# A two-layer graph kernel on one core: X W's table in partition order, fewer early rows of A, and other cuts of two strip loads

## The chip, the cores and the metric

The kernel runs on one core of a Trainium2 chip. The metric is the time of one execution on the device in microseconds (us); the median of several runs is taken. A profiled execution gives the trace that the tables and rows below come from.

The engines have short names in all views: PE is TensorE (matmuls), DVE is VectorE, ACT is ScalarE, POOL is GpSimd and SP is SyncE. Loads and stores are issued by an engine's queue (POOLq, SPq, ACTq) and carried out by 16 DMA engines.

## The reference

There are N = 2708 nodes with D = 128 features, and A is the 0/1 adjacency matrix. Layer 0 adds a diffusion and an attention over cosine similarities, and layer 1 is a graph attention in which the softmax-like weights are normalised by a product with A:

```python
# layer 0
deg = clip(A.sum(1), 1);  dis = deg ** -0.5
diffusion = (dis[:, None] * A * dis[None, :]) @ x - x
attn = softmax(beta * cos(x, x) * A, axis=1)
x = layernorm(x + diffusion + sigmoid(alpha) * (attn @ x - x))
# layer 1
XW = X @ W
s_col, s_row = XW @ a[0, :128], XW @ a[0, 128:]
den = exp(leaky_relu(s_row[:, None] + s_col[None, :], 0.01))
num = A @ den
att = where(num != 0, den / num, 0)
H = A @ (att @ XW)
out = layernorm(X + layer1)      # layer1 = H
```

Everything is float32. The kernel gets x, A (`adj`) and A transposed (`adj_t`), with rows padded with zeros to 2816.

## The kernel before, in words

The nodes are cut into `NB` = 22 blocks of 128 rows, and the columns of A into `NS` = 6 strips of `SW` = 512, of which the last, strip 5, is 148 wide. The work goes through five stages in the trace's time: the attention of layer 0 (0 to 217 us), the diffusion (217 to 306), scores and tables (306 to 362), the main loop (362 to 575), and H with the output (575 to 681).

**The diffusion.** The loop runs over the strips in the order 0, 5, 1, 2, 3, and strip 4 follows behind it. `diffuse` multiplies one strip by x, block by block. Strips 1 to 4 (`RAISED`) are multiplied by two rounded parts of x (`x_hi`, `x_lo`), strips 0 and 5 by `x_sb`, the tile that holds x. Behind each strip come the layernorm, two scores (`sb_ps`), and small work on DVE that tallies them. A strip is loaded by `load_strip` in two DMAs of 11 blocks each, strips 1 to 4 on POOL's queue and strips 0 and 5 on SP's. There are three rooms: `strip_a` holds strips 0, 2 and 4 in turn, `strip_b` strips 1 and 3, and `strip_c` strip 5. So strip s + 2 is loaded once `diffuse(s)` has ended.

**The sums over rows of A.** Separately, `tot` collects sums over the rows of A with weights that come from the scores. The first three strips' columns (`KEPT`) are no longer at hand when the weights are known, so those columns are loaded again, 768 KB for each block of rows; this is `first_strips`, with 12 matmuls for each block. The other columns are read from the strips that remain (`kept_strips`). `fill` with a pattern of "e" (first) and "k" (kept) places such blocks of work by hand between other work on PE. The tiles for "e" rotate through five rooms: the room of x (`x_sb`), and those of the four halves of `x_hi` and `x_lo`. Three early blocks have a pool of their own, `early_nat`, and are summed behind the strips 1, 2 and 3; a fourth, in `x_sb`, follows behind strip 3.

**The order of the instructions.** Up to the end of the diffusion, a scheduler at build time orders the instructions of each engine. From `strict.append("end of the diffusion")` on, PE, DVE, ACT and POOL keep the written order (`pinned`).

**The tables.** `project` makes X W, and `store_xw` writes it to a scratch table in device memory (`xw_d`, one row of 128 numbers for each node) in two DMAs on ACT's queue. The nodes are sorted into up to `NG` = 24 groups of `G` = 126. One-hot products (`onp`, `k_ons`, `j_ons`, `tab_ps`) turn the order into lists of row numbers: `k_no` for the rows of A and `j_no` for the rows of X W. A list's values are sums in which an absent entry is 0, so each number carries an offset (`from_n`) that `rows_of_table` takes off again. `gather(g)` then loads the rows of A of group g by an indirect DMA on POOL's queue, into a ring of four rooms of which the first is `x_sb` again, and `gather_xw(g)` loads the rows of X W.

**The main loop** runs over the groups: a product (`num`), a logarithm, a division, a power, and a product that collects `m_acc`. Then H = A·M is made in rounded parts. A slower path for other data (`general`) is in the program and is not executed.

Of the kernel before, what the change touches and what calls it, by code (L numbers as in the profile page):

```python
# [9 lines left out]
F32 = mybir.dt.float32  # L10
# [4 lines left out]
ALU = mybir.AluOpType  # L15
# [3 lines left out]
P = 128  # L19
N = 2708  # L20
D = 128
NB = (N + P - 1) // P
NP = NB * P
LAST = N - (NB - 1) * P
SW = 512
# [7 lines left out]
NG = 24  # L33
# [4 lines left out]
LAG = 2  # L38
TAIL = (NS - 1) * SW
PARTS = ((0, 1024), (1024, 2048), (TAIL, N), (2048, TAIL))  # L40
EARLY_ROWS = 3
RAISED = (1, 2, 3, 4)
KEPT = 3
LIMIT = 16.0
# [5 lines left out]
def grouped(  # L50
# [14 lines left out]
    nc = tc.nc  # L65

    def pool(name, bufs=1, space=None, side="left", stack=ctx):
        kw = {"space": space} if space else {}
        return stack.enter_context(
            tc.tile_pool(name=name, bufs=bufs, side=side, reuse_waits="tile", **kw)  # L70
        )
# [4 lines left out]
    def width(s):  # L76
        return min(SW, N - s * SW)

    def blocks(s):
        return min(SW // P, NB - s * (SW // P))  # L80
# [35 lines left out]
    def counted(name, pattern, base, step, size):  # L116
        t = const.tile([P, size], F32, name=name)
        nc.gpsimd.iota(
            t, pattern, base=base, channel_multiplier=step,
            allow_small_or_imprecise_dtypes=True,  # L120
        )
        return t
# [12 lines left out]
    nc.gpsimd.memset(going[:, :, 0], 0.0)  # L135
    pad = const.tile([P, NB], F32, name="pad")
    from_n = const.tile([P, NB], F32, name="from_n")
    after_node = const.tile([P, 2], F32, name="after_node")

    row0, row1, half_on, rest, head = (  # L140
# [35 lines left out]
    def pinned(engine, op, *args, **kwargs):  # L176
        with ExitStack() as e:
            if engine in latest:
                e.enter_context(tc.issue_after(latest[engine].ins))
            latest[engine] = op(*args, **kwargs)  # L180
            return latest[engine]
# [9 lines left out]
    def dve(op, *args, **kwargs):  # L191
        if strict:
            return pinned("DVE", getattr(nc.vector, op), *args, **kwargs)
        return getattr(nc.vector, op)(*args, **kwargs)  # L194
# [109 lines left out]
    att = lp.tile([P, NB, D], F32, name="att")  # L304
# [3 lines left out]
    with ExitStack() as es:  # L308
# [196 lines left out]
        for n, s in enumerate(order):  # L505
# [48 lines left out]
            for k, jb in enumerate(blocks_j):  # L554
# [26 lines left out]
                if m == n:  # L581
                    for o in range(n):
                        if (o, n) in rooms:
                            _, tag = rooms.pop((o, n))
                            (free if tag.startswith("room") else free_small).append(tag)
                if m > n:
                    if (n, m) not in rooms:
                        few = order[m] == NS - 1
                        tag = (free_small if few else free).pop(0)
# [44 lines left out]
                if n == NS - 1 and k in (7, 13, 18, 21):  # L634
# [4 lines left out]
                    while done:  # L639
                        b0 = b1 = done[0]  # L640
# [13 lines left out]
    es = ExitStack()  # L654
# [1 line left out]
    strip_b = pool("strip_b", stack=l0)  # L656
    strip_c = pool("strip_c", stack=l0)
    nat = pool("nat", stack=l0)
    early_nat = pool("early_nat", stack=es)
    work2 = pool("work2", 2, stack=es)  # L660
    tots = ExitStack()
    ps_tot = pool("ps_tot", 1, PSUM, side="right", stack=tots)
# [49 lines left out]
    def sum_part(part, bank, q, kb, c, rows):  # L712

        mm(
            nc.tensor.matmul, tot[32 * q : 32 * q + 2, bank, c : c + rows.shape[-1]],
            e2_w[:, part, kb, :], upper(rows), start=(bank, q) not in begun, stop=False,
            tile_position=(0, 32 * q), skip_group_check=True,
        )
        begun.add((bank, q))

    summed = [*range(16), 20, 21, 16, 17, 18, 19]

    def first_strips(kb, eng):
        room = (summed.index(kb) - EARLY_ROWS) % 5
        if kb < EARLY_ROWS:
            a = early_nat.tile([P, KEPT * SW], F32, tag="nat", name="nat")
        elif room == 0:
            a = x_sb.rearrange("p b d -> p (b d)")[:, : KEPT * SW]
        else:
            tag = (None, "x_hi0", "x_lo0", "x_hi1", "x_lo1")[room]  # L730
            a = nat.tile([P, KEPT * SW], F32, tag=tag, name="nat")
        eng.dma_start(a, adj_t[ts(kb, P), : KEPT * SW])
        for part in range(3):
            for q in range(4):
                sum_part(part, 0, q, kb, 0, a[:, ts(q, quarters[0])])

    kept_parts = []
    for q in range(4):
        i, end = KEPT * SW + q * quarters[1], KEPT * SW + (q + 1) * quarters[1]
        c = 0  # L740
        while i < end:
            s = min(i // SW, NS - 1)
            n = min(end, s * SW + width(s)) - i
# [3 lines left out]
    def kept_strips(kb, eng):  # L747
# [2 lines left out]
                sum_part(part, 1, q, kb, c, strips[s][:, kb, i : i + n])  # L750

    jobs = {
        "e": [(first_strips, kb) for kb in summed[EARLY_ROWS:]],
        "k": [(kept_strips, kb) for kb in summed],
    }

    def fill(pattern):

        for c in pattern:
            f, kb = jobs[c].pop(0)  # L760
            f(kb, nc.sync)
# [44 lines left out]
    def load_strip(s):  # L806
        v = width(s)
        t = homes[s].tile(
            [P, NB, v if s == NS - 1 else SW], F32R if s in RAISED else F32, tag="strip",
            name=f"strip{s}",  # L810
        )
        src = adj_t[:, s * SW : s * SW + v].rearrange("(b p) i -> p b i", p=P)
        for h0, h1 in ((0, NB // 2), (NB // 2, NB)):
            q = nc.gpsimd if s in RAISED else nc.sync
            q.dma_start(t[:, h0:h1, :v], src[:, h0:h1, :])
        strips[s] = t
# [46 lines left out]
    def scores(s, x1_t, k, pb):  # L863

        mm(
            nc.tensor.matmul, pb[:, : blocks(s) * P], wa_bc[:, k, :],
            x1_t[:, : blocks(s) * P], start=True, stop=True,
        )
        return pb
# [42 lines left out]
    def store_xw(s0, s1):  # L912
        b0, b1 = s0 * 4, min(s1 * 4, NB)
        nc.scalar.dma_start(
            xw_d[b0 * P : b1 * P, :].rearrange("(b p) d -> p b d", p=P), att[:, b0:b1, :]
        )

    def score_bank():
# [2 lines left out]
    for s in (0, 5, 1, 2, 3):  # L921
        v, nb = width(s), blocks(s)
        acc = ps_acc.tile([P, SW], F32, tag="acc", name="dif_acc")
        diffuse(s, acc)
        if s < 3:
            load_strip(s + 2)
        if s == 0:
            attended(*ended)
        h = mixed(s, turned(to_sbuf(acc, v, nb), nb, ps_tp))
        to_x1(s, h, *moments(h, nb))  # L930
        x1_t = x1_in_sbuf(s, x1_turned(s))
        pbs = []
        for k in (1, 0):
            pb = scores(s, x1_t, k, score_bank())
            tally(s, pb, k)
            pbs.append(pb)
        shared_row(s, pbs[0])
        picked(s, pbs[0], sr_p)
        picked(s, pbs[1], sc_p)
        limited(s * 4, s * 4 + nb)  # L940
        e2(s * 4, s * 4 + nb)

        if s in (1, 2, 3):
            first_strips(s - 1, nc.sync)
        if s == 3:
            fill("e")


    s = NS - 2
# [2 lines left out]
    strict.append("end of the diffusion")  # L952
    h_s = mixed(s, turned(to_sbuf(acc, SW, 4), 4, ps_tp))
    to_x1(s, h_s, *moments(h_s, 4))
    fill("keekk")
    tp = x1_turned(s)
    fill("k")
    x1_s = x1_in_sbuf(s, tp)
# [151 lines left out]
    def valued(name, k, hot, val, b0=0, b1=NB):  # L1110

        for b in range(b0, b1):
            act(
                "activation", ons[name][:, k, b, :NG], hot[:, :, b], AF.Identity,
                scale=val[:, b : b + 1],
            )

    def valued_by_dve(name, k, hot, val):
        dve(
            "tensor_tensor", ons[name][:, k, :, :NG].rearrange("p b g -> p g b"), hot,  # L1120
            along(val, NG, NB), ALU.mult,
        )
# [21 lines left out]
    def table(name, onp, v, o, p0, between):  # L1144

        t = tmp.tile([P, 1, P], F32, tag=name + "_t", name=name + "_t")
        partial_table(name, onp, v, o)
        act("copy", t[:, 0, :], o)
        between()
        return selected(name, t, [v], p0)  # L1150

    def banks(*tags):
        return [
            ps_x.tile([P, SW], F32, tag=tag, name="tab_ps", bufs=2)[:, :P] for tag in tags
        ]

    def rows_of_table(name, o, n):
        idx = tab.tile([P, NG], mybir.dt.uint32, name=name + "_no")
        dve("tensor_scalar", idx[:n], o[:n, 0, :], float(N), None, ALU.add)
        return idx  # L1160


# [32 lines left out]
    k_onp = placed("k", k_own)  # L1195
    j_hot = grouped_by("j", j_gt)
    k_tab = table("k", k_onp, 0, *banks("x"), P - G, lambda: fill("kke"))
    valued("k", 1, k_hot, low, 17)
    valued("j", 1, j_hot, cs_p, 0, 12)
    j_run, j_ahead, j_of = numbered("j", j_hot)  # L1200
    valued_by_dve("j", 0, j_hot, from_n)
    k_no = rows_of_table("k", k_tab, G)
    k_tab = table("k", k_onp, 1, *banks("x"), 0, lambda: fill("eee"))
    valued("j", 1, j_hot, cs_p, 12)
    assert not any(jobs.values()), jobs
    tmp.tile([P, P], F32, name="spare")
    j_own = chosen("j", j_hot, j_run, j_ahead)
# [109 lines left out]
    def numbers():  # L1317

        o = ps_num.tile([P, SW], F32, tag="num", name="j_sel")
        for v in range(2):  # L1320
            mm(
                nc.tensor.matmul, o[:, ts(v, NG)], j_t[:, v, :], four[:, :NG],
                start=True, stop=True,
            )
        idx = rows_of_table("j", o[:, :NG].unsqueeze(1), P)
        dve("tensor_copy", c_s, o[:, NG : 2 * NG])
        dve("tensor_scalar", nc_s, c_s, -1.0, None, ALU.mult)
        return idx
# [82 lines left out]
    for step in range(NG + LAG):  # L1411
        g, before, first = step, step - 1, step - LAG
# [82 lines left out]
    k = NG  # L1495
# [70 lines left out]
    for p0, p1 in PARTS:  # L1566
# [4 lines left out]
        for kb in range(0, NB, step) if p0 != TAIL else (0,):  # L1571
            n = min(step, NB - kb)
# [8 lines left out]
            else:  # L1581
                n = NB
# [13 lines left out]
            if p0 == PARTS[0][0] and kb in (3 * step, 6 * step):  # L1596
                b0 = len(lasts) * NB // 2
# [456 lines left out]
```

## Time and profile before

| what | value |
|---|---|
| time, median of 3 runs | 688.89 us (686.5 to 692.6) |
| the profiled execution | 682.83 us, of which the span of the core is 681.1 us |
| mean granted PE clock | 0.975 |
| busy: PE, DVE, ACT, POOL | 92%, 72%, 71%, 36% of the span |
| DMA, mean over the span | 264 GB/s, 179.9 MB |
| strip loads on POOL's queue | 8 DMAs of 2,816 KB, median 20.0 us from issue to landing |
| strip 5's loads on SP's queue | 2 DMAs of 814 KB, landing 11.0 and 21.0 us after issue |
| rows of A for `first_strips` | 768 KB each, median 6.9 us from issue to landing |

The busy shares are averages over stages with different limits, so they do not say what a change in one stage is worth. Three kinds of rows do: the chain of waits (what ended last, in order of time, with start and length), the list of what an engine waited for, and the timeline of one engine with the idle time before each group of instructions in brackets. All times in rows count from the start of the span.

### The profile page before, as it was taken

How to read it: one execution, taken by the hardware profiler on the slowest of the kernel's cores; microseconds unless marked ns; L12 is line 12 of the kernel's file. 1: busy time of each engine (PE TensorE's matmuls, PEld its weight loads, DVE VectorE, ACT ScalarE, POOL GpSimd, SP SyncE). 2: the span in 40 equal slices, each digit the busy share in tenths (PEclk: the TensorE clock that was granted, in tenths of full speed). 3: DMA queues.
4: the chain of work that ended last, by engine and by line, in shares of the span. 5: the costliest groups of instructions: out<-in, count | busy, mean ns of one | idle time of the engine just before them, and what ended most of it. 6: DMA issues, size and time to landing. Idle time of an engine off the chain costs nothing.

```text
span 681.1 us, 8586 instructions
## 1 busy us (share of the span) xinstructions
PE 627.2 (92%) x2859; PEld 356.1 (52%) x2859; DVE 491.0 (72%) x1003; ACT 482.3 (71%) x670; POOL 246.2 (36%) x246
## 2 busy tenths in 40 slices
PE   7999999999999999888867999999999999969883
PEld 4445453545546576556653444444444445657752
DVE  5776876657555455577776999999999996767473
ACT  4767777777874013222576999999999999578772
POOL 5976788788975201000124222222222400100011
PEclk9999999999997999999979999999999999979996
DMA  8958989998989999987969984444444633399990
GB/s 278 336 188 291 356 311 346 337 315 315 300 279 368 341 395 390 390 262 297 348 228 243 241 235 157 151 152 161 162 165 168 193 121 111 107 381 378 403 340 24
DMA packets 67910, 179.90 MB, mean 264 GB/s; under 512 B 6794, under 2 KB 18724, under 8 KB 64836
## 3 DMA queue, kind: packets, MB, share of 16 engines
q1 hardware_dynamic: 47092, 117.33, 48.8%
q0 software_dynamic: 16816, 60.19, 28.5%
q10 hardware_dynamic: 3952, 1.77, 0.9%
q8 instruction: 24, 0.39, 0.2%
q14 instruction: 26, 0.21, 0.1%
HBM read 176.44 MB, written 2.84 MB: 263 GB/s over the span
## 4 chain that ended last, share of the span: by engine, by line
PE 64%; DMA 12%; issue 12%; DVE 5%; ACT 4%; POOL 2%; ACTq 0%; DVEq 0%; POOLq 0%
PE num L180 15%; PE m_acc L180 15%; PE att_acc L189 12%; PE sim L189 9%; DMA strip<-in_adj_t 8%; PE dif_acc L189 4%; DMA xw_d<-att 2%; DMA beta_sb<-in_beta 1%; PE tot L180 1%; PE sim L180 1%; DVE q L180 1%; DMA row<-in_adj 1%; ACT xn L180 1%; PE m_tail L180 1%; PE att_acc L180 1%
## 5 line engine op out<-in xcount | busy, mean ns | idle before, releaser
L205 POOL TENSOR_TENSOR total<-total,p_t 128x512 f32<-128x512 f32 (+3 forms) x111 | 125.1, 1128 | 35.6 <-ACT p_t L199 30.3
L180 PE MATMUL m_acc<-q,xws 128*128 128x512 f32 x240 | 121.6, 592 | 0.0
L194 DVE SCALAR_TENSOR_TENSOR p_t<-sim,gentle,piece 128x512 f32<-128x512 f32 (+1 forms) x111 | 72.0, 670 | 48.6 <-PE sim L189 39.7
L180 PE MATMUL num<-ring,wt 128*128 128x512 f32 x216 | 98.1, 546 | 2.9 <-DVE q L180 2.2
L189 PE MATMUL att_acc<-p_t,x_sb 128*128 128x512 f32 (+1 forms) x228 | 97.7, 555 | 2.3 <-ACT p_t L199 2.1
L199 ACT ACTIVATE p_t<-p_t,shift 128x512 f32<-128x512 f32 (+1 forms) x111 | 69.2, 655 | 34.6 <-DVE p_t L194 29.1
L180 DVE SCALAR_TENSOR_TENSOR q<-sr_b,nc_s,q 128x1536 f32<-128x1536 f32 (+1 forms) x48 | 77.8, 1623 | 16.6 <-ACT q L180 16.5
L180 DVE COPY q<-num 128x512 f32<-128x512 f32 (+1 forms) x142 | 83.5, 611 | 3.7 <-PE num L180 3.7
L180 PEld LDWEIGHTS m_acc<-q,xws 128*128 128x128 f32 x240 | 45.3, 190 | 55.0 <-issue 54.8
L180 ACT ACTIVATE q<-q,head,rest 128x1536 f32<-128x1536 f32 (+1 forms) x48 | 70.2, 1508 | 1.5 <-DVE ring L180 1.2
L180 ACT ACT_TABLE_LOAD x52 | 66.7, 1283 | 3.8 <-issue 2.9
L189 PEld LDWEIGHTS att_acc<-p_t,x_sb 128*128 128x128 f32 x228 | 41.0, 202 | 45.1 <-ACT p_t L199 24.7
L180 PEld LDWEIGHTS num<-ring,wt 128*128 128x128 f32 x216 | 39.0, 190 | 48.2 <-issue 34.2
L180 ACT ACTIVATE row<-row 128x1354 f32<-128x1354 f32 x44 | 58.2, 1323 | 8.1 <-DMA row<-in_adj 8.1
L180 ACT ACTIVATE q<-q,c_s 128x1536 f32<-128x1536 f32 (+1 forms) x48 | 62.9, 1355 | 0.3
L1589 PE MATMUL h_acc<-rounded,m_hi 128*128 128x512 f32 (+1 forms) x132 | 45.8, 409 | 14.9 <-DVE rounded L1508 14.2
L180 POOL DMA_INDIRECT ring<-in_adj_t,k_no x18 | 22.6, 1256 | 93.4 <-PE num L180 92.5
L189 PE MATMUL sim<-xn_t 128*128 128x512 f32 (+1 forms) x102 | 47.4, 582 | 0.0
L1513 ACT ACTIVATE junk<-ring 128x2048 int16<-128x2048 int16 (+1 forms) x21 | 39.3, 1870 | 5.0 <-DMA ring<-in_adj_t 4.6
L1589 PE MATMUL h_acc<-rounded,m_lo 128*128 128x512 f32 (+1 forms) x132 | 42.8, 393 | 0.0
L189 PE MATMUL dif_acc<-strip,x_hi 128*128 128x512 f32 x88 | 36.8, 418 | 3.9 <-DMA strip<-in_adj_t 3.9
L1589 PEld LDWEIGHTS h_acc<-rounded,m_hi 128*128 128x128 f32 x132 | 25.1, 201 | 23.4 <-DVE rounded L1508 18.1
(315 smaller groups left out, 1018.9 us busy)
## 6 DMA issues: line engine op xcount, KB each, us to landing
row<-in_adj SPq DMA_DIRECT2D x44, 677.0 KB, 5.3
piece<-in_adj_t SPq DMA_DIRECT2D x24, 1024.0 KB, 6.4
strip<-in_adj_t POOLq DMA_DIRECT2D x8, 2816.0 KB, 20.0
ring<-in_adj_t SPq DMA_DIRECT2D x20, 1024.0 KB, 7.8
nat<-in_adj_t SPq DMA_DIRECT2D x18, 768.0 KB, 6.9
x_sb<-in_adj_t SPq DMA_DIRECT2D x7, 1024.0 KB, 8.3
strip<-in_adj_t SPq DMA_DIRECT2D x2, 2816.0 KB, 15.3
piece<-in_adj_t SPq DMA_DIRECT2D x7, 512.0 KB, 6.6
```

Source lines behind the costliest of these rows:

```text
L180: latest[engine] = op(*args, **kwargs)
L189: op(*args, **kwargs)
L194: return getattr(nc.vector, op)(*args, **kwargs)
L199: return getattr(nc.scalar, op)(*args, **kwargs)
L205: getattr(nc.gpsimd, op)(*args, **kwargs)
L1513: nc.scalar.activation(junk[:, :n], low, AF.Abs, accum_out=low_bits[:, i : i + 1])
L1589: nc.tensor.matmul(acc[:, : h1 - h0], m[:, kb + b, :], rows_r[b][:, h0:h1], start=(kb + b, part) == (0, 0), stop=(kb + b, part) == (NB - 1 ...
```

## The change

The table `xw_d` is written with the row of node b·128 + p at place p·22 + b, so each partition's rows lie together. The row numbers in `j_no` follow: the one-hot values of the rows come from a new constant, `from_row`, instead of `from_n`, and the offset of an absent entry is that of a row that is empty (461).

The pool `early_nat` goes. The first two blocks of `first_strips` both use the room of x, and the rotation over five rooms starts behind them. They are summed behind the strips 1 and 3, one each, so two blocks instead of four lie in the diffusion. The other two are placed in the patterns behind it: "keekk" becomes "keeekk", and "eee" becomes "ee" with another "ee" further on.

Strip 1 is loaded in one DMA of 22 blocks, and strip 4 in three, of 8, 8 and 6 blocks. The other strips keep their halves.

```diff
-EARLY_ROWS = 3
...
+    empty = LAST * NB + NB - 1
+    from_row = counted("from_row", [[1, NB]], -empty, NB, NB)
...
-    early_nat = pool("early_nat", stack=es)
...
     def first_strips(kb, eng):
-        room = (summed.index(kb) - EARLY_ROWS) % 5
-        if kb < EARLY_ROWS:
-            a = early_nat.tile([P, KEPT * SW], F32, tag="nat", name="nat")
-        elif room == 0:
+        room = max(summed.index(kb) - 1, 0) % 5
+        if room == 0:
             a = x_sb.rearrange("p b d -> p (b d)")[:, : KEPT * SW]
...
-        "e": [(first_strips, kb) for kb in summed[EARLY_ROWS:]],
+        "e": [(first_strips, kb) for kb in summed],
...
-        for h0, h1 in ((0, NB // 2), (NB // 2, NB)):
+        cuts = {1: (0, NB), 4: (0, 8, 16, NB)}.get(s, (0, NB // 2, NB))
+        for h0, h1 in zip(cuts, cuts[1:]):
             q = nc.gpsimd if s in RAISED else nc.sync
             q.dma_start(t[:, h0:h1, :v], src[:, h0:h1, :])
...
-            xw_d[b0 * P : b1 * P, :].rearrange("(b p) d -> p b d", p=P), att[:, b0:b1, :]
+            xw_d.rearrange("(p b) d -> p b d", p=P)[:, b0:b1, :], att[:, b0:b1, :]
...
-        if s in (1, 2, 3):
-            first_strips(s - 1, nc.sync)
-        if s == 3:
+        if s in (1, 3):
             fill("e")
...
-    fill("keekk")
+    fill("keeekk")
...
-    def rows_of_table(name, o, n):
+    def rows_of_table(name, o, n, first=N):
         idx = tab.tile([P, NG], mybir.dt.uint32, name=name + "_no")
-        dve("tensor_scalar", idx[:n], o[:n, 0, :], float(N), None, ALU.add)
+        dve("tensor_scalar", idx[:n], o[:n, 0, :], float(first), None, ALU.add)
...
-    valued_by_dve("j", 0, j_hot, from_n)
+    valued_by_dve("j", 0, j_hot, from_row)
     k_no = rows_of_table("k", k_tab, G)
-    k_tab = table("k", k_onp, 1, *banks("x"), 0, lambda: fill("eee"))
+    k_tab = table("k", k_onp, 1, *banks("x"), 0, lambda: fill("ee"))
     valued("j", 1, j_hot, cs_p, 12)
+    fill("ee")
...
-        idx = rows_of_table("j", o[:, :NG].unsqueeze(1), P)
+        idx = rows_of_table("j", o[:, :NG].unsqueeze(1), P, empty)
```

## The prediction

> **What bounds the kernel now.** I read the 40 slices of the page first: PE is at 8 or 9 tenths nearly throughout, so a microsecond counts where PE, or the engine that feeds it, stands still. The change touches three places: the diffusion over strips (217 to 306 us), the tables (306 to 362) and the start of the main loop (362 on). For each I read the chain of waits, which says what ended last:
>
> ```profile
> 238.34 27.01 DMA strip<-in_adj_t
> 265.35 0.04 issue
> 265.39 4.23 PE dif_acc L189 x17
> ...
> 272.61 26.02 DMA strip<-in_adj_t
> 298.62 0.04 issue
> 298.67 0.50 PE dif_acc L189
> ...
> 329.22 13.05 DMA xw_d<-att
> ```
>
> Three loads carry 66 us of the chain. That is not what they cost; PE's waits over 200 to 312 us say what they cost (total, times, longest):
>
> ```profile
> PE dif_acc L189 <- DMA strip<-in_adj_t: 4.8, 4, 2.2
> PE x_ps L180 <- DVE x L180: 1.8, 1, 1.8
> ```
>
> Only 4.8 us: 0.96 for strip 5 at 241.8, then 0.25, 2.22 and 1.39 for strips 2, 3 and 4. PE and DMA run level here; the DMA engines move 350 to 410 GB/s through 222 to 298. PE's timeline (start, length, what, idle before) shows who waits for whom at the start:
>
> ```profile
> 223.93 13.04 PE L189 MATMUL dif_acc<-strip,x_sb 128*128 128x512 f32 x30
> ...
> 238.37 2.43 PE L189 MATMUL dif_acc<-strip,x_sb 128*128 128x148 f32 x18
> 241.76 0.52 PE L189 MATMUL dif_acc<-strip,x_sb 128*128 128x148 f32 x2 [0.96 <-DMA strip<-in_adj_t]
> ```
>
> and POOL's, on whose queue strips 1 to 4 are loaded:
>
> ```profile
> 219.40 1.36 POOL L815 DMA_DIRECT2D strip<-in_adj_t  x1 [1.75 <-DVE p_t L194]
> ...
> 237.28 2.15 POOL L815 DMA_DIRECT2D strip<-in_adj_t  x2 [12.22 <-PE dif_acc L189]
> ```
>
> The 512-wide matmuls are strip 0, the 148-wide ones strip 5. Strip 0 ends at 236.99, and its end releases the load of strip 2 into the same room at 237.28. Strip 5's halves, issued at 220.3 and 220.7, land at 231.3 and 241.7 (814 KB takes 10 us because strip 1 comes in at the same time). PE reaches the second half at 240.8 and waits 0.96 us.
>
> **The order on PE.** Nothing in the diff names it, but outside the strict parts a scheduler orders the instructions, and the built order of the changed kernel differs: PE runs 14 of strip 0's 22 blocks, then 11 of strip 5's, then strip 5's second half, and only then strip 0's last 8. In before's times: a block of strip 0 costs 0.859 us (13.04 / 15 with the overlap), one of strip 5 0.243. The 14 blocks end at about 230.1. Strip 5's first half lands at 231.3: **1.2 us** of wait. Eleven blocks take 2.7, to 234.0. The second half lands at 241.7: **7.7 us** of wait, with the 8 blocks that used to fill it (6.9 us) behind it in PE's queue. Strip 0 then ends at about 250 instead of 237, so strip 2 is issued at 250 to 252.5 instead of 237.3, and the DMA queue, empty from about 246, stands still some 6 us.
>
> A stall of 7.7 us also costs clock. At 597.7 to 603.3 PE idled 5.60 us; the columns of these windows are sum, PE, PEld, DVE, ACT, POOL, granted clock, DMA share, GB/s:
>
> ```profile
> 602.00:603.00 1.00, 0.00 (x0) 0.00 (x0) 1.00 (x2) 0.97 (x3) 0.00 (x0) 0.52 1.02 422
> ...
> 607.00:608.00 1.00, 1.00 (x4) 0.81 (x3) 1.00 (x3) 1.00 (x1) 0.00 (x0) 0.50 1.00 385
> 608.00:609.00 1.00, 1.00 (x4) 0.77 (x4) 1.00 (x2) 0.97 (x3) 0.00 (x0) 0.57 1.09 410
> 609.00:610.00 1.00, 1.00 (x6) 0.82 (x5) 1.00 (x2) 1.00 (x1) 0.00 (x0) 1.00 0.91 348
> ```
>
> Half clock for 5.5 us after work resumed; after idles of 4.36 us (at 341) and 2.55 us (at 667) it was 4.1 and 3.5 us, mean 4.4. Half of that is lost: **2.2 us**. The Trainium skill, "TensorE: Matmul & The Clock Gate", section "HAM oscillation — how this bites in real kernels", rules out idle gaps over about 3.4 µs, and its Part 1 puts the warm-up at the same 3.4 µs; by that I would estimate 1.7 us. The rule speaks against this change, since the new gap is over twice its limit; I take the rows, which show longer recoveries, a drop already after 2.55 us, and none after the 2.2 us at 279.8.
>
> **The other parts.**
> - *Early rows.* Two rows of A instead of four are summed in the diffusion. A row is 12 matmuls and costs 0.68 us of PE: −1.4 there. The two return in the tables, where PE waits: one before the transposes of strip 4 (PE stood 1.76 us for DVE's x, the second wait above), one behind the second table. Cost 0 while those waits last, 1.4 if not. Of their loads, 0.79 MB each, one leaves the tail of strip 5's queue and the others move behind; at 2.0 us a row they make room in the strips' queue.
> - *Cuts.* Strip 1 in one load is complete when its second half was, 245.9. In before's order PE started it at 244.99 and would wait 0.9; in the new order it starts at about 250, so 0. Issuing: the row nearest is a 22-block load with 1.79 us against 1.36 + 1.11 for two halves; POOL is idle, so 0. Strip 4 in three: the last piece is 6 blocks instead of 11, landing no later. Nothing else waits on POOL's queue.
> - *Strips 2 to 4, all later.* At 7.3 us a half (2.88 MB) from 252.3, strip 2 lands at 261.6 and 268.9, strip 3 at 278 and 286 to 287.5, strip 4 by 302 to 303. PE, itself late, needs the second half of strip 3 at about 290 and the last piece at about 305: margins of 2 to 3 us. So the old waits 0.25, 2.22, 1.39, and the 0.96, go: −4.8. A short new wait of 0.6 stands behind strip 3, and strip 3's scores (4.55 us of DVE) now stand 8 matmuls from the end and push strip 4's h by about 0.45.
> - *Table in partition order.* The two stores go from pieces of 512 B to 6,144 and 5,120 B per partition. The chain gives the second 13.05 us, but who waits for it is DVE, and barely:
>
> ```profile
> 342.39 3.09 DVE L180 TENSOR_TENSOR onp<-k_at,col 128x2816 f32<-128x2816 f32 x1 [1.14 <-DMA xw_d<-att]
> ```
>
>   DVE had work to 341.25. So the gain lies between 0 and **1.1 us**; by bytes at 390 GB/s the store would be done by about 335, so I take −1.1. The loads of rows beside it keep their time. The gathers from the table read the same 512-B rows: 0. The new iota lies in POOL's idle time at the start, 0.16 us for its like.
> - *The last row's room.* Row 21 now lies in x_sb, where the first gather puts its rows. In before:
>
> ```profile
> 351.13 1.17 POOL L180 DMA_INDIRECT x_sb<-in_adj_t,k_no  x1 [20.63 <-DVE k_no L180]
> ...
> 352.61 1.07 POOL L180 DMA_INDIRECT ring<-in_adj_t,k_no  x1 [0.30 <-issue]
> ```
>
>   Released by the numbers alone. Now it also waits for row 21's 12 matmuls, the last on PE before j's table: about 3.5 us behind k_no, so 353.5 where 350.0 was possible. The next gathers wait behind it on POOL, and come 7 to 8 us apart (359.3, 367.2, 374.2). Their slack was 3.0 us for group 0 (wanted at 362.31), 0.9 for group 1 (368.08). Group 1 lands at about 369.7, 1.7 us late against before and 2.7 against the chain that the store moved. ACT sets the loop (8.86 us a step, 199 of 201 us busy), so its start passes on whole; part of the delay falls into ACT's early waits. Bounds 0 and 2.7; I take +1.5, so with the store +0.4.
>
> **Sum**, against the profiled execution (682.83 us; span 681.1). Diffusion: 1.2 + 7.7 + 2.2 + 0.6 − 1.4 − 4.8 = +5.5; walking stage by stage, where part of the half-clock stretch lies under work that waits anyway, gives +4.4. I take +4.6, so it ends near 310.8. Then +0.45 and +0.4: **+5.5**, 688.3. The median of the runs shown, 688.89, lies 6.1 above that execution; on it the forecast is **694.4**, with its own range 691 to 698.
>
> **Rivals.**
> 1. *No stall* (0.12). Strip 5's second half is there by 234.0, since strip 1, as one load, shares the engines otherwise. Then the diffusion ends 3.3 us early (old waits 4.8 and rows 1.4 go, some 2.9 come back as the wait for strip 1 and behind it), DVE and gather add 0.9: −2.4, **686.5**. Against it: the same bytes are asked for at the same instants (219.4, 220.3), and 241.7 was measured so.
> 2. *DMA becomes the bound* (0.24). From 252 three strips and the rows, 18 to 19 MB, must come in 52 us with margins of 2 to 3. If a half takes over 8 us, as beside row loads (7.3 + 2.0), strip 3 or 4 is late by 3 us, and the gathers by 1 more: +9.5, **698.4**. For it: 2.22 and 1.39 us waited in before.
> 3. *The store was on the path* (0.04): the chain's 13.05 us shrink to the 5.0 that the first store took, and the tables move up by all 8.05 instead of 1.1: +5.5 − 6.95 = −1.4, **687.5**. Against it: DVE's 1.14, behind which nothing was ready.
>
> The forecast keeps 0.60. About 1% (6.9 us) is what a measurement of this kernel can tell from no change. The forecast's range reaches past it at its upper end, so it gives a good quarter of its 0.60 to slower; rival 2 gives nearly all of its 0.24 there; rivals 1 and 3 lie within 1%, with their lower tails beyond. Faster 0.05, same 0.55, slower 0.40. The range 686.5 to 701.5 holds the forecast and most of rivals 1 and 2.
>
> **What will show it.** Right: one wait of 7 to 8 us of PE before a 128x148 dif_acc, granted clock 0.50 behind it, strip 2 issued near 251, the four old waits gone, DVE's wait for xw_d gone, and the first gather released by PE and about 3.5 us behind k_no. Wrong: no such wait (rival 1), or waits of 3 us and more before strips 3 and 4 (rival 2), or the main loop starting over 2 us off the shift of the diffusion's end.

## The result, and the profile after

Over 20 runs of each kernel the median went from 686.78 us (680.12 to 692.6) to 692.06 us (687.53 to 698.4). The ratio is 1.0083, 95% interval 1.0056 to 1.011: 5.7 us slower, which is clear of no change and under 1%. The ratio leaves out executions over 1.5% above the fastest of their kernel: one of each kernel here, one of *halves4* and four of *rows_only* below. The forecast was 694.4 from 688.89, which is +5.5. Its starting point was the median of three runs; over 20 runs the kernel before lies 2.1 us lower, so the measured 692.06 is 2.3 us below the forecast although the difference agrees to 0.2 us.

The profiled execution after took 692.68 us, with a span of 691.0 us. That is 9.9 us above the first profiled execution before, and not all of it is the change. Both kernels were profiled a second time (before2 and after2 below), and the stages, each counted from the end of the one ahead of it, read so:

| stage, us | before | before2 | after | after2 |
|---|---|---|---|---|
| start to strip 0's first matmul (attention) | 217.42 | 219.54 | 220.22 | 217.62 |
| to strip 4's first h on DVE (diffusion) | 90.17 | 90.51 | 95.52 | 93.33 |
| to k_no (scores, sorting, k's table) | 43.03 | 45.38 | 42.68 | 42.45 |
| to the first num (j's table, first gather) | 11.69 | 12.63 | 13.89 | 12.34 |
| to the loop's first power on ACT | 10.75 | 12.44 | 12.35 | 10.72 |
| main loop, to the last power | 203.03 | 203.04 | 203.01 | 213.11 |
| H and output, to the end of the span | 105.01 | 104.86 | 103.33 | 105.03 |
| span | 681.1 | 688.4 | 691.0 | 694.6 |

The attention, which the edits leave alone, took 217.4 to 220.2 us in these four and is no part of the answer. The diffusion is longer after the change in both pairs. The rows from k_no on vary for reasons that the experiments below take apart.

PE's waits over the diffusion in the changed kernel:

```profile
PE dif_acc L190 <- DMA strip<-in_adj_t: 7.9, 3, 6.9
PE att_acc L190 <- ACT p_t L200: 2.2, 2, 1.9
PE tot L181 <- DMA nat<-in_adj_t: 1.2, 1, 1.2
```

Before there were four waits for strips, none over 2.2 us. Now one of 6.9 is nearly all of it. PE's timeline shows where it stands:

```profile
226.73 8.94 PE L190 MATMUL dif_acc<-strip,x_sb 128*128 128x512 f32 x36
242.54 1.85 PE L190 MATMUL dif_acc<-strip,x_sb 128*128 128x148 f32 x6 [6.87 <-DMA strip<-in_adj_t]
...
245.35 9.75 PE L190 MATMUL dif_acc<-strip,x_sb 128*128 128x512 f32 x22
```

A row of the timeline names the first of its matmuls. The first row's 36 go on from strip 0 (14 matmuls) into strip 5's first half (22) without a gap. Then PE stands 6.87 us for strip 5's second half. Its first three blocks (six matmuls) come next, then strip 0's last eight blocks (16 of the 22 matmuls in the last row), and then the rest of strip 5. So three blocks of strip 5's second half stand ahead of strip 0's end, and not all eleven as the prediction has it; its "about 250" for that end fits three (241.7 + 0.7 + 6.9). POOL's queue pays for that:

```profile
222.19 1.64 POOL L814 DMA_DIRECT2D strip<-in_adj_t  x1 [1.74 <-DMA strip<-in_adj_t]
...
254.66 2.20 POOL L814 DMA_DIRECT2D strip<-in_adj_t  x2 [27.59 <-PE dif_acc L190]
```

Strip 2 is issued 34.4 us after strip 0's first matmul (254.66 − 220.22), where it was 19.9 before. In the windows around the stall (the columns are those of the windows in the prediction) the clock goes down in the idle time and stays there after work resumes at 242.5, and the DMA engines run dry:

```profile
239.00:240.00 1.00, 0.00 (x0) 0.00 (x0) 0.00 (x0) 0.00 (x0) 0.00 (x0) 0.53 1.21 367
240.00:242.00 2.00, 0.00 (x0) 0.00 (x0) 0.00 (x0) 0.00 (x0) 0.00 (x0) 0.50 1.25 403
242.00:244.00 2.00, 1.46 (x6) 1.46 (x7) 0.00 (x0) 0.00 (x0) 0.00 (x0) 0.50 1.26 418
...
248.00:249.00 1.00, 1.00 (x3) 0.48 (x2) 0.00 (x0) 0.00 (x0) 0.00 (x0) 0.50 0.02 6
249.00:250.00 1.00, 1.00 (x3) 0.40 (x3) 0.00 (x0) 0.00 (x0) 0.00 (x0) 0.85 0.00 0
250.00:251.00 1.00, 1.00 (x4) 0.47 (x3) 0.00 (x0) 0.00 (x0) 0.00 (x0) 1.00 0.00 0
```

The chain of waits of the changed kernel tells the same at both ends of the diffusion:

```profile
223.50 19.00 DMA strip<-in_adj_t
...
242.54 1.85 PE dif_acc L190 x6
...
314.06 1.69 DVE picked L195 x16
315.75 0.08 DVE low L195
315.83 1.03 DVE h L181 x4
```

Strip 5's second half comes 19.0 us after its issue, and PE goes on within the same row. At the end DVE's own work for strip 3 (picked, low) is what strip 4's h waits for, and no longer PE.

In the tables DVE's wait for the store is gone; the row of k's placement has no bracket of idle time any more:

```profile
349.38 3.09 DVE L181 TENSOR_TENSOR onp<-k_at,col 128x2816 f32<-128x2816 f32 x1
```

The first gather is released by PE's sums, not by the numbers, and PE waits for it (POOL's rows, then PE's):

```profile
363.02 1.47 POOL L181 DMA_INDIRECT x_sb<-in_adj_t,k_no  x1 [24.54 <-PE tot L181]
```

```profile
372.31 3.58 PE L181 MATMUL num<-x_sb,wt 128*128 128x512 f32 x4 [2.45 <-DMA x_sb<-in_adj_t,k_no]
```

k_no came at 358.42, so the gather stood 4.6 us behind it. The four matmuls took 3.58 us, at half clock; in the first profile before they took 1.98, but in before2, where the gather was in time, 3.67. So the wait belongs to the late gather, and the half clock here does not belong to it alone.

### The profile page after: what moved, and what is told of

The parts are those of the page before. It is cut to its first block, busy times and chain, and to the rows that moved or that the text cites. A ratio compares the mean times of both kernels' runs of the same rounds, so it can differ in the third digit from the quotient of the medians.

```text
span 691.0 us, 8584 instructions
## 1 busy us (share of the span) xinstructions
PE 632.1 (91%) x2859; PEld 358.6 (52%) x2859; DVE 490.9 (71%) x1003; ACT 482.5 (70%) x670; POOL 244.6 (35%) x247
## 4 chain that ended last, share of the span: by engine, by line
PE 62%; issue 12%; DMA 12%; DVE 7%; ACT 5%; POOL 2%; DVEq 0%; SPq 0%; POOLq 0%; ACTq 0%
PE num L181 15%; PE m_acc L181 15%; PE att_acc L190 9%; PE sim L190 7%; DMA strip<-in_adj_t 6%; PE dif_acc L190 5%; DMA row<-in_adj 4%; PE tot L181 2%; ACT row L181 2%; DMA x_sb<-in_adj_t,k_no 1%; PE idle_ps L181 1%; PE sim L181 1%; DVE q L181 1%; ACT xn L181 1%; PE m_tail L181 1%
## 5 line engine op out<-in xcount | busy, mean ns | idle before, releaser
L181 DVE SCALAR_TENSOR_TENSOR q<-sr_b,nc_s,q 128x1536 f32<-128x1536 f32 (+1 forms) x48 | 77.8, 1624 | 16.5 <-ACT q L181 16.4
L190 PEld LDWEIGHTS att_acc<-p_t,x_sb 128*128 128x128 f32 x228 | 40.8, 201 | 46.8 <-ACT p_t L200 26.2
L1587 PE MATMUL h_acc<-rounded,m_hi 128*128 128x512 f32 (+1 forms) x132 | 44.2, 395 | 15.0 <-DVE rounded L1506 14.4
L181 POOL DMA_INDIRECT ring<-in_adj_t,k_no x18 | 21.2, 1178 | 93.4 <-PE num L181 92.5
L1587 PE MATMUL h_acc<-rounded,m_lo 128*128 128x512 f32 (+1 forms) x132 | 40.9, 378 | 0.0
L181 PE MATMUL num<-x_sb,wt 128*128 128x512 f32 (+1 forms) x72 | 34.4, 570 | 2.5 <-DMA x_sb<-in_adj_t,k_no 2.5
## 6 DMA issues: line engine op xcount, KB each, us to landing
row<-in_adj SPq DMA_DIRECT2D x44, 677.0 KB, 5.6
```

What stands on the lines that cost most here:

```text
L1587: nc.tensor.matmul(acc[:, : h1 - h0], m[:, kb + b, :], rows_r[b][:, h0:h1], start=(kb + b, part) == (0, 0), stop=(kb + b, part) == (NB - 1 ...
```

## The experiments

**Which edit makes the stall.** Two loads were cut anew, and the order on PE differs in two places. Strip 5 moves ahead of the end of strip 0, and strip 3's scores, which stood 17 matmuls ahead of strip 4's end, stand 6 ahead of it. Three runs ask which load does which, and what each order costs.

*held*: the changed kernel, with only PE's order put back. `held[s]` keeps the latest matmul of strip s, and the first matmul of strip 5 is issued behind strip 0's last.

```diff
...
+                    if s == 5 and jb == 0:
+                        e.enter_context(tc.issue_after(held[0].ins))
...
```

> The changed kernel, with the first matmul of strip 5 held behind the last of strip 0, so PE runs strip 0's 22 blocks first, as before the change; strip 1 stays in one load. Theory A (the order on PE is the price): the wait of 6.9 us and the half clock behind it go; PE waits 1 to 2 us for strip 5 and about 1 us for strip 1 instead, strip 2 is issued as strip 0 ends, about 20 us after strip 0's first matmul instead of 34. Time 5 to 6 us below the changed kernel, ratio to before 1.000 to 1.003. Theory B (the loads themselves, strip 1 in one piece and the strips behind it, are the price): the wait moves to strip 1 or to strips 2 to 4, 5 us or more in sum, and the ratio stays at 1.006 to 1.010.

Measured: 683.42 us, ratio to before 0.9955 (0.9926 to 0.9984). The wait is gone, and so are all other waits for strips; PE runs from strip 0 into strip 5 with no idle time, and strip 2 is issued 20.5 us after strip 0's first matmul:

```profile
241.06 4.95 PE L832 MATMUL dif_acc<-strip,x_sb 128*128 128x148 f32 x38
```

```profile
240.20 2.20 POOL L814 DMA_DIRECT2D strip<-in_adj_t  x2 [13.18 <-PE dif_acc L832]
```

The diffusion took 83.4 us to strip 4's h, 6.8 less than in before's first profile and 12 less than in the changed kernel's. So theory A holds, and more than its 5 to 6 us came back (8.8 by the ratios): with the order kept, the cuts do no harm, and every strip is there when PE asks for it.

*cut1_before*: the kernel before with one edit, strip 1 in a single load.

```diff
-        for h0, h1 in ((0, NB // 2), (NB // 2, NB)):
+        cuts = {1: (0, NB)}.get(s, (0, NB // 2, NB))
+        for h0, h1 in zip(cuts, cuts[1:]):
```

> The kernel before with one edit: strip 1 in one load of 22 blocks. Its built order on PE has strip 5 ahead of strip 0's last 8 blocks, as in the changed kernel. Theory A (this one line, through the order, makes the stall): PE waits 6 to 7.5 us for strip 5's second half and runs at half clock behind it, strip 2 is issued 31 to 34 us after strip 0's first matmul instead of 20, and the ratio to before is 1.007 to 1.012 (the stall with the four early rows still in the diffusion, and no store's gain). Theory B (another part of the change causes it, or the stall is paid back by shorter waits for the later strips): ratio 0.998 to 1.004.

Measured: 691.23 us, ratio 1.0093 (1.0067 to 1.012), +6.4 us.

```profile
PE dif_acc L189 <- DMA strip<-in_adj_t: 8.3, 4, 6.7
```

```profile
251.66 2.19 POOL L816 DMA_DIRECT2D strip<-in_adj_t  x2 [25.88 <-PE dif_acc L189]
```

One wait of 6.7 us, and strip 2 issued 32.7 us after strip 0's first matmul (218.94). One line, with no word on the order of matmuls, costs as much as the whole change.

*halves4*: the changed kernel with strip 4 in two halves.

```diff
-        cuts = {1: (0, NB), 4: (0, 8, 16, NB)}.get(s, (0, NB // 2, NB))
+        cuts = {1: (0, NB)}.get(s, (0, NB // 2, NB))
```

> The changed kernel, with strip 4 in two halves again (strip 1 stays in one load). In the built order strip 3's scores then stand 16 matmuls before strip 4's end instead of 6. Theory A (the three pieces cost through the order at the end): DVE's tail behind strip 4 shortens by 2.0 to 2.3 us (10 matmuls of 0.2335), PE waits at most 0.5 us more for strip 4's second half, ratio to before 1.004 to 1.007. Theory B (the three pieces spare a wait for strip 4): PE waits 1.4 us or more for the second half, and the ratio is 1.008 to 1.010.

Measured: 693.91 us, ratio 1.0106 (1.0068 to 1.0144). Not faster, and not clearly slower than the changed kernel's 1.0083. Strip 3's scores stand 16 matmuls ahead of the end again, so strip 4's three pieces had moved them. The diffusion took 94.2 us, between the changed kernel's two profiles (95.5 and 93.3), so the order at the end is worth nothing that shows; PE waits instead for x of strip 3 (1.8 us). Neither theory is confirmed: A's gain is not there, and for B PE's waits for strips besides the stall come to 0.7 us, not 1.4. What was not expected stands on ACT:

```profile
ACT wt L181 <- DMA wt<-g_d: 7.1, 1, 7.1
```

This is a load of 252 KB of weights, which ACT takes up in the third step of the main loop. Here it took 28.6 us, and the loop 212.2 us instead of 203.0.

**The room of the last row.** *row21*: the changed kernel, with the last row block's tile in another room.

```diff
         room = max(summed.index(kb) - 1, 0) % 5
+        if kb == summed[-1]:
+            room = 1
```

> The changed kernel, with row block 21's last tile in the second room instead of x's, so that the first gather need not wait for its matmuls. Theory A (the room is a price of its own): the first gather is issued within 0.5 us of k_no instead of 4.6 us behind, PE's wait of 2.45 us for it and the half clock behind that go, and the main loop starts 3 to 4 us earlier; ratio to before 1.003 to 1.005. Theory B (the row in the second room comes later and holds j's table by as much, or the gathers are late for another reason): the main loop starts within 1 us of the changed kernel's, ratio 1.007 to 1.009.

Measured: 689.9 us, ratio 1.0043 (1.0023 to 1.0064), by the ratios 2.7 us below the changed kernel. The first gather is released by the numbers again, 0.5 us behind k_no (353.12):

```profile
353.62 1.18 POOL L181 DMA_INDIRECT x_sb<-in_adj_t,k_no  x1 [19.96 <-DVE k_no L181]
```

PE's wait for the gather is gone too. The half clock at the first num is not (3.63 us for four matmuls); PE still idles in front of it, for DVE and ACT. Theory A's ratio holds, but not its claim on the clock, and its place for the gain does not show: from k_no to the loop's first power it took 25.1 us here, and 26.2 and 23.1 in the changed kernel's two profiles. A part of the 2.7 us may be the late weights, below.

**The parts alone.** *store_only*: the kernel before with the table part. Its edit is the table's lines of the diff.

> The kernel before with the table part alone. Theory A (DVE's wait for the store, 1.14 us, is all that goes): ratio 0.997 to 0.9995, 1 to 1.5 us at the start of the main loop, no more. Theory B (the 13 us of the store on the chain were path): 5 us or more at the start of the main loop, ratio 0.990 to 0.993. Theory C (nothing, since the wait moves to k's table): ratio 0.9995 to 1.001.

Measured: 679.94 us, ratio 0.9928 (0.9898 to 0.9958), −4.9 us. That lies in theory B's range, but the trace does not show B: from h to k_no it takes 42.5 us, 0.5 less than in before's first profile and 2.9 less than in its second, and everything behind k_no is as in the first. The diffusion, ahead of the store, was 1.6 us shorter (two waits for strips, 3.7 us, instead of four with 4.8), and no line of this edit touches that stage. Of the 3.5 us between the two profiles, 2.6 lie ahead of the store.

*nostore* asks the same question in another place: the version with both prices repaired (held_row21, below), with the old table order (the row numbers go back to `from_n` with it).

```diff
...
-            xw_d.rearrange("(p b) d -> p b d", p=P)[:, b0:b1, :], att[:, b0:b1, :]
+            xw_d[b0 * P : b1 * P, :].rearrange("(b p) d -> p b d", p=P), att[:, b0:b1, :]
...
```

> The version with both prices repaired (strip 5 held behind strip 0, row 21 in the second room), with the table in its old order: the two stores in pieces of 512 B again. Theory A (the store is worth DVE's wait for it): DVE waits 1 to 1.5 us for xw_d before k's placement, the main loop starts about 1 us later, ratio to before 0.989 to 0.992, against 0.988 with the new order. Theory B (the store is worth what the store alone brought, 5 us): ratio 0.994 to 0.997, and the trace shows 4 us or more between the store and the end of the main loop.

Measured: 677.68 us, ratio 0.99 (0.9865 to 0.9935), against 0.9883 (0.9848 to 0.9918) with the new order. The intervals overlap, 1.2 us apart. The ratio is in theory A's range; the wait in this profile, 4.3 us, is larger than A had. It passes on whole: from h to k_no it takes 46.0 us here and 41.7 in held_row21. DVE's list of waits in this kernel, and in before's second profile:

```profile
DVE onp L181 <- DMA xw_d<-att: 4.3, 1, 4.3
```

```profile
DVE onp L180 <- DMA xw_d<-att: 3.4, 1, 3.4
```

In the six profiles with the table's old order DVE waited for the store 1.1, 3.4, 0.9, 0 and 0.7 us, and 4.3 here, where DVE is ready earlier; in the eight with the new order it never did. So the gain is not a fixed 1.1 us: by these profiles it is what DVE has to wait in that execution, 1.7 us in the mean. The two longest waits are from long runs (690.23 us, and 684.27 where the median is 677.68), so 1.7 may be high for a middling one. Why store_only measured 4.9 is not settled.

*rows_only*: the kernel before with the early rows' part.

> The kernel before with the rows part alone: two early rows in x's room, row 21 last in x's room. The start's order is that of before. Theory A: the diffusion ends 2 to 3 us earlier (two rows 1.4 us, and shorter waits for strips), the first gather comes 3.5 to 4.6 us behind k_no, which takes 2 to 3 us back at the main loop: ratio 0.998 to 1.001. Theory B (the rows are hidden in the diffusion, since strips arrive no earlier): diffusion as before, gather late, ratio 1.003 to 1.006.

Measured: 684.39 us, ratio 0.9987 (0.9966 to 1.0007). The ratio is theory A's: no difference that shows. Its reason is half seen. The gather comes 4.4 us behind k_no (360.65 and 356.20), as in the changed kernel. But the diffusion does not end earlier in this profile: it took 93.1 us, with waits of 2.4 and 2.1 us for strips. The profile is of one of the longest runs (694.95 us, median 684.39), so it does not speak for the others. ACT waited for the weights in it as well:

```profile
ACT wt L179 <- DMA wt<-g_d: 4.1, 1, 4.1
```

**The repairs together.** *best*: both cuts undone, and row 21 in the second room by the two lines of *row21*.

```diff
-        cuts = {1: (0, NB), 4: (0, 8, 16, NB)}.get(s, (0, NB // 2, NB))
+        cuts = (0, NB // 2, NB)
```

> The changed kernel with both cuts undone (all strips in halves) and row block 21 in the second room; what stays is the table in partition order and the two early rows. Theory A: the start's order is that of before, no stall, the tail and the gather's wait are gone, the store's 1.1 us and two rows (1.4 us of PE in the diffusion, partly behind strip waits) are gained: 1 to 2 us below before, ratio 0.996 to 0.999. Theory B (the rows cost when they come back in the tables, or loads of rows there delay others): ratio 1.001 to 1.004.

Measured: 681.16 us, ratio 0.9896 (0.9865 to 0.9927), −7.1 us, more than theory A had. In this profile, of the longest of its six runs (682.0 us), the diffusion took 88.0 us. Strip 2's, 3's and 4's old waits are gone even with all strips in halves, with two early rows (1.6 MB) less to load; in *rows_only*, with the same loads, one of 2.1 us was left. One wait is left here, the one for strip 5; below it the same matmuls in *store_only*:

```profile
243.49 4.46 PE L190 MATMUL dif_acc<-strip,x_sb 128*128 128x148 f32 x20 [1.92 <-DMA strip<-in_adj_t]
```

```profile
241.85 2.78 PE L191 MATMUL dif_acc<-strip,x_sb 128*128 128x148 f32 x20 [2.02 <-DMA strip<-in_adj_t]
```

The 20 matmuls take 4.46 us, at half clock, behind 1.92 us of idle time, and 2.78 us, at full clock, behind 2.02 us. The last section has the reason that the traces suggest.

*held_row21*: both repairs on the changed kernel, cuts and all.

```diff
...
+        if kb == summed[-1]:
+            room = 1
...
+                    if s == 5 and jb == 0:
+                        e.enter_context(tc.issue_after(held[0].ins))
...
```

> The changed kernel with strip 5's first matmul held behind strip 0's last, and row 21's last tile in the second room: all parts of the change without their two prices. Theory A (the prices add up, and the cuts gain where the order is kept): no wait for any strip, the end of the diffusion as in the held kernel, some 6 us earlier against strip 0's first matmul than before, the gather directly behind k_no; ratio 0.985 to 0.992. Theory B (with the tables reached earlier, DVE or the loads of rows set the main loop's start, so the two repairs do not add): ratio 0.992 to 0.996.

Measured: 677.03 us, ratio 0.9883 (0.9848 to 0.9918), −8.0 us. The diffusion took 83.8 us with no wait for a strip, and the gather follows k_no by 0.5 us:

```profile
344.86 1.18 POOL L181 DMA_INDIRECT x_sb<-in_adj_t,k_no  x1 [19.48 <-DVE k_no L181]
```

It beats the kernel before and the changed one, and can't be told from *best* by its time.

**The spread.** *wt_split*: the kernel before, with the 252 KB of weights in four loads.

```diff
-    spread_out_weights(4, 8)
+    for g in range(4, 8):
+        spread_out_weights(g, g + 1)
```

> The kernel before, with the first load of weights from g_d (groups 4 to 7, 252 KB) cut into four loads of one group. In the traces so far this load took 6 to 29 us beside the gathers, and ACT waited 4 and 7 us for it where it took over 24. Theory A (this wait falls into a good part of all executions and makes their spread and part of the store's apparent gain): ratio 0.993 to 0.998, and the slowest runs of this kernel lie 2 us or more below before's. Theory B (a rare event): ratio 0.998 to 1.002, spread as before.

Measured: 685.25 us, ratio 1.001 (0.999 to 1.003). Theory B: in the kernel before this wait is rare. The first piece landed in 3.6 us.

*before2* and *after2*: second profiled executions.

> The kernel before, once more, for a second profiled execution. Theory A (the first one, 682.83 us against a median of 686.8, had none of the random waits): the attention ends at 217 to 220 us and ACT may wait for weights; 684 to 688 us. Theory B (profiled executions are always that fast): 682 to 684 us.

> The changed kernel, once more, for a second profiled execution. Theory A (the difference of 9.9 us between the two first profiled executions holds 2.8 us of the attention, which the change leaves alone): counted from strip 0's first matmul to the end, 470 to 472 us again, and the time before it anywhere from 215 to 221. Theory B: the attention is slower with the change, 220 us again.

Measured: 690.23 us (span 688.4) and 696.33 us (span 694.6). The first is above the range of either theory: the spans of before's two profiles lie 7.3 us apart. The attention was slower in before's second profile and faster in the changed kernel's, so its 2.8 us were chance. From strip 0's first matmul to the end the changed kernel took 677.0 us this time, not 470 to 472 (694.6 − 217.62). One row explains the 6 us and more:

```profile
ACT wt L181 <- DMA wt<-g_d: 10.0, 1, 10.0
```

Taking all 13 profiles together in which this load is one piece: with the first gather behind row 21 (the changed kernel twice, held, halves4, rows_only) ACT waited for these weights 0, 10.0, 0, 7.1 and 4.1 us; with the gather directly behind k_no (the other eight) it waited 1.3, 0.2 and otherwise 0. Where ACT waits, the main loop is longer by the wait or somewhat more (213.1, 212.2, 207.3 and 204.5 us for 10.0, 7.1, 4.1 and 1.3, against 203.0). The load is issued 15.9 to 16.4 us behind the first gather in the five, and 18.7 to 20.5 us in the eight; it took 10.4 to 28.6 us in the five and 5.6 to 22.5 in the eight. That points to the late gather as the cause, but it is counting and no experiment: splitting the load in a kernel with the late gather was not tried.

## Why the prediction was right, point by point

**The stall.** Predicted 1.2 + 7.7 us, at strip 5's two halves; measured 0 and 6.87 (6.03 in after2). The first half was there when PE asked, and the second took 19.0 us where before's trace had 21, so the term was 2 us too large, and that was no chance. With strip 1 in one load and strip 5 moved ahead, the second half let PE go on 21.5 to 22.3 us after strip 0's first matmul in five profiles; with strip 1 in halves it was 24.2 to 25.7 us in six. So the landing was not independent of strip 1's cut, as the prediction argued against rival 1; that rival's reason was at work, but it was worth 2 to 3 us and not the whole stall. Its consequences came as told: strip 2 predicted at 250 to 252.5, and 254.66 − 2.80 of slower attention = 251.9 in before's times. *held* and *cut1_before* show that this order is the price, from both sides.

**The clock.** Predicted 5.5 us at half speed in the row shown, 4.4 in the mean, and 2.2 us lost. Measured from the resumption to the return of full clock in the five profiles with this stall: 6.8 us here, 4.6 in after2, 3.6 in cut1_before and halves4, 3.9 in row21; mean 4.5, so 2.2 lost. The time at half speed varies almost twofold between executions of the same order, and here it was at the long end. The rows had the mean right, where the 3.4 µs of the rule that the prediction quotes (the Trainium skill, "TensorE: Matmul & The Clock Gate", Part 1) gives 1.7 us.

**The old waits.** Predicted to go with 4.8 us; measured 0.27 and 0.79 left in the changed kernel's first profile, 0.78 in its second. The new wait of 0.6 behind strip 3 is there as 0.62. The margins for strips 3 and 4 held, so rival 2, at 698.4, did not come. *No stall* (rival 1, as a total) fell with the 6.87.

**The diffusion in sum.** Predicted +4.6, and +0.45 for DVE's tail; measured +5.35 from the first pair of profiles and +2.8 from the second. (PE's transposes for strip 4 ended at 314.9 in the changed kernel and h began at 315.7, so DVE's tail was 0.85; strip 3's scores stood 6 matmuls from the end and not 8.) In the first profile the stall was 2.0 us below its term and the clock cost 3.4 instead of 2.2, which cancel in part; in the second the stall was 2.9 below and the clock, with 2.3, at its term, and nothing cancels.

**The store.** Predicted −1.1 with a bound of 0 to 1.1 taken from one profile. This is a term whose size failed: the wait was 0 to 4.3 us in six profiles, so the bound was that of one execution. Rival 3, the full 8 us, fell all the same: store_only gained 4.9 and the comparison of nostore with held_row21 gives 1.2.

**The gather.** Predicted 3.5 us behind k_no and +1.5; measured 4.6 behind, PE's wait for the gather 1.0 to 2.5 us in the five profiles that have it late (none in the other nine), and 2.7 us of time by *row21*. The working had the gather for group 1 as the late one; it was that for group 0, whose slack of 3.0 us was used up by a longer wait behind PE's sums and a landing of 9.2 us instead of 8.2. And it left out ACT's wait for the weights, which in three of these five profiles was 4 to 10 us.

**What stays open.** The parts do not add: +6.4 for the one load, −0.9 for the rows and −4.9 for the store make +0.6, and +5.7 was measured. With 1.7 for the store, the mean of DVE's waits, the sum is +3.8, and each of these differences is uncertain by 1.4 to 2.1 us, so the store's 4.9 is the part that fits least. Another possible reason is that the rows gain by shortening waits for strips that the stall removes as well, and each wait goes only once; no run separates this. The late weights are a third. The remainder, and the 4.9 of the store, are not explained by these runs. So the order on PE and its stall were foreseen, but the total came out within 0.2 us with errors of 1 to 3 us in single terms in both directions, which is partly luck.

## What to carry to other kernels

Where a scheduler orders the instructions, look at the built order on each engine before pricing an edit: here the number of pieces of one load moved another strip's matmuls ahead of work that used to hide their load, and holding that order, with the last row's room changed, turned a loss of 5.7 us into a gain of 8.0. When the last tile of a rotation lands in a room that a later, critical load needs, that load inherits the tile's wait, and whatever is queued behind it does too. A wait that is read off one profile is one draw: take a second profile before using it as a bound, and look where the profiled run lies among the others.

## What the runs showed of the hardware that was not expected

In the 14 profiles the granted clock fell to half and came back 81 times. Each of these stretches lasted 3.41, 6.83 or 10.24 us, which is one, two or three times 3.41. Within a profile all falls and returns lie whole multiples of 3.413 us apart, to 0.02 us. In the changed kernel's first profile they stand at 204.93, 215.16, 239.06, 249.29, 351.69, 358.52, 372.18, 375.59, 614.52 and 617.93 us. So the clock changes only at instants of a fixed beat. In *best* it even fell after PE had resumed at 243.49, and it came back 3.41 us later; a window with a mean between 0.50 and 1.00 holds the change:

```profile
244.00:244.25 0.25, 0.25 (x5) 0.25 (x4) 0.00 (x0) 0.00 (x0) 0.00 (x0) 0.89 1.21 401
...
247.50:247.75 0.25, 0.25 (x3) 0.25 (x3) 0.00 (x0) 0.00 (x0) 0.00 (x0) 0.78 1.24 459
```

So the length of an idle time alone does not say what it costs, and its place against the beat may be why. The 1.92 us of *best* lay whole between two instants of the beat (240.78 and 244.19), and so did 2.36 us in *rows_only*; behind both the clock fell. The 2.02 us of *store_only* and the 2.2 us at 279.8 in the first profile of before were each cut by an instant (at 241.14 and 281.18) into parts of at most 1.4 us, and the clock stayed up. That is a reading of four cases, which no run tested. It is not the whole rule either: between 202 and 206 us the clock fell in 13 profiles although PE was busy by the trace throughout the 3.41 us before.

At the first num of the main loop the same four matmuls took either 1.96 to 1.98 us (5 of 14 profiles) or 3.4 to 3.7 us (9), in kernels with the gather early and late, and the stretch from there to the loop's first power was then 1.4 to 1.7 us longer. So a part of the spread between runs can be where an idle time falls against this beat.

A load of 252 KB that spreads rows of 504 B over all partitions took between 5.6 and 28.6 us beside gathers of whole rows of A.
